# An expert's four activations as one run, beside the last attention unit of layers 1 and 3

## The chip, the core and the metric

The kernel is one program on one core of a Trainium2 chip. It is measured as device time in microseconds (us) of one execution. The engines that matter here each work through a queue of their own in order: PE (matrix products into the PSUM banks), ACT (activation functions, copies out of PSUM), DVE (elementwise work and reductions), POOL and SP (here mostly issuing DMAs). They wait for each other through semaphores.

## What is computed

A token array x of 1024 tokens by 128 features goes through four layers, each a cross attention against a context of 6404 rows and a feed-forward block, both added to x. The two blocks that the change touches are the feed-forward blocks of layers 1 and 3, mixtures of 8 experts that are all computed in full for all tokens:

```
L1:  h = gelu(einsum('bsh,ehf->ebsf', x, w1) + b1)        # E=8, H=128, F=512
     y = einsum('ebsf,efh->ebsh', h, w2) + b2
     out = einsum('ebsh,bse->bsh', y, one_hot(argmax(x @ wr + br)))
...
L3:  h = gelu(einsum('nd,edf->enf', x, w1) + b1)          # 8 experts, D=128, F=512
     res = x + einsum('enf,efd->end', h, w2) + b2
     normed = (res - mean) * rsqrt(var + 1e-6)            # per expert
     y = einsum('end,ne->nd', normed * gamma + beta, gates)   # gates: softmax of the top 2
```

The attention of layers 1 and 3 has 16 heads of 8 features with a softmax over the 6404 context rows.

## The kernel before, in words

The 1024 tokens are handled in two halves of 512. The attention of layers 1 and 3 (`attn_softmax`) runs over 16 units: 8 pairs of heads times two halves. A unit goes through its 51 blocks of 128 keys in 26 steps of two blocks, which makes four score tiles of 128 keys by 512 queries in a step (two blocks, two heads). What is issued in which order is written out by hand: PE, ACT and DVE are in a manual schedule, in which each engine's queue has the order in which the Python code emits the instructions. The order of a step is a string:

```
order = ("SMSMSP", "SMSMP", "SMSMSP")
```

Each letter is a slot. **S** makes scores: by turns an x tile (two score tiles in two banks, one buffer) or a y tile (one bank, one buffer), by the products of L1121, and then their Exp on ACT (L1126, into px or py). An S can be issued on PE only once the Exp of the last tile of its kind has read the bank. **P** multiplies the weights of the step before with the values (L1012). **M** is a slot for other work. In the units before the last it takes the search for the score maxima of a later unit (L893, L897). In the last unit there is no later unit, and M advances two generators instead: `beside` (layer 1 only: the keys of layer 2, `heads_keys`), and from step 9 of the unit on `also`, the feed-forward block of the first half of the tokens, which is ready by then. Each `yield` of that block is the end of an M slot. So the experts of the first half run between the pieces of the last unit, with two M slots to a step; what is left of them is emitted behind the unit's last P, between the pieces of its end (`finish`: copy of the bank at L1020, the division by the softmax sum at L1034, projection).

One call of `expert` does one expert (L1154 on). It asks for a weight tile (two, taken by turns), issues the DMAs of w1 and w2 (L1160, L1161) on SP, and then handles the 512 hidden features in two parts. For each part it makes two first products of 128 features by 512 tokens into banks of `h_tile` (a pool of two buffers in the last unit), each followed by its Gelu on ACT with the bias (L1184), into a hidden tile (two, by turns). In the trace the products are L1183 (two PE instructions each) and the hidden and weight tiles of this place are called kb, since they lie in the storage of the keys' tile. After a `yield`, the function calls what waits in a list; after one more `yield` it puts the part's second products (`second`, L1172: 8 products as 16 PE instructions, summed in one bank of `m_tile`, of which there are two) into that list. The slots of expert e are therefore: part 0; the second part of the second products of expert e-1, and its adding to x on DVE; part 1; the first part of the second products. The adding is `add_weighted` in layer 1 (L627) and `add_normed` in layer 3 (L1702 to L1716, a layer norm per expert, with one power on POOL at L114). With expert 0's adding goes a bias term (`bias`): four transposes (L607), a DVE copy (L608), eight small products (L620) and a DVE add (L614).

ACT holds one set of function tables at a time. Between an Exp and a Gelu, and back, stands an ACT_TABLE_LOAD, which has the line of the activation that needs it.

The second half of the tokens goes through the same `expert` outside the attention (`experts_apart`), with tile pools of three weight and three hidden tiles; no manual schedule is used there.

Of the kernel before, what the change touches and what calls it, by code (L numbers as in the profile page):

```python
# [10 lines left out]
F32 = mybir.dt.float32  # L11
# [4 lines left out]
AF = mybir.ActivationFunctionType  # L16
# [4 lines left out]
P = 128  # L21
S = 1024
NT = S // P
HALF = 512
# [11 lines left out]
def done(steps):  # L36

    while True:
        try:
            next(steps)  # L40
        except StopIteration as end:
            return end.value


class Net:
# [1104 lines left out]

    def expert(self, L, e, xnT, w_tile, hidden_tile, waiting):

        nc = self.nc
        w = w_tile()
        w1, w2 = w[:, :512], w[:, 512:].rearrange("p (k d) -> p k d", d=D)
        nc.sync.dma_start(out=w1, in_=self.a[f"L{L}_ffn_w1"][e])  # L1160
        nc.sync.dma_start(  # L1161
            out=w2, in_=self.a[f"L{L}_ffn_w2"][e].rearrange("(k f) d -> f k d", f=P)
        )
        got = {}

        def second(part, hid):
            if part == 0:
                got["y"] = self.m_tile()
            y = got["y"]
            for i in range(HT):  # L1170
                for k in range(2):
                    nc.tensor.matmul(  # L1172
                        y[:, ts(i, P)], hid[:, k, ts(i, P)], w2[:, 2 * part + k],
                        start=part == 0 and i == 0 and k == 0,
                        stop=part == 1 and i == HT - 1 and k == 1,
                    )

        for part in range(2):
            hid = hidden_tile()
            for j in range(2):  # L1180
                k = 2 * part + j
                h = self.h_tile()
                nc.tensor.matmul(h, w1[:, ts(k, P)], xnT, start=True, stop=True)  # L1183
                nc.scalar.activation(  # L1184
                    hid[:, j], h, AF.Gelu, bias=self.col(f"L{L}_b1", 4 * e + k)
                )
            yield
            while waiting:
                waiting.pop(0)()
            yield  # L1190
            waiting.append(lambda part=part, hid=hid: second(part, hid))
        return got

    def ffn1(self, half, pool, w_tile, hidden_tile):
        nc, a = self.nc, self.a
        E = 8
        wr = pool.tile([P, E], F32, name="wr")
        br = pool.tile([P, E], F32, name="br")
        b2 = pool.tile([E, D], F32, name="b2")
        nc.sync.dma_start(out=wr, in_=a["L1_ffn_wr"])  # L1200
        nc.sync.dma_start(out=br, in_=a["L1_ffn_br"].partition_broadcast(P))
        nc.sync.dma_start(out=b2, in_=a["L1_ffn_b2"])
        xn, xnT = yield from self.normed(half)
        sc = pool.tile([P, HT, E], F32, name="sc")
        nc.vector.tensor_tensor(
            sc, self.router(xnT, wr, E), br.unsqueeze(1).to_broadcast([P, HT, E]), ALU.add
        )
        cw = self.ranks_below(pool, sc, E, 1)
        waiting = []

        def bias():
            self.add_projected(self.weights_transposed(pool, cw, E), b2, half)

        for e in range(E):
            got = yield from self.expert(1, e, xnT, w_tile, hidden_tile, waiting)
            waiting.append(lambda got=got, e=e: self.add_weighted(got["y"], half, cw, e))
            if e == 0:
                waiting.append(bias)
        while waiting:
            waiting.pop(0)()  # L1220
            yield
# [455 lines left out]

    def ffn3(self, half, pool, w_tile, hidden_tile):  # L1680
        nc, a = self.nc, self.a
        E = 8
        wr = pool.tile([P, E], F32, name="wr")
        beta = pool.tile([E, D], F32, name="beta")
        nc.sync.dma_start(out=wr, in_=a["L3_ffn_router_w"])
        nc.sync.dma_start(out=beta, in_=a["L3_ffn_beta"])
        xn, xnT = yield from self.normed(half)
        lg = pool.tile([P, HT, E], F32, name="lg")
        nc.vector.tensor_copy(lg, self.router(xnT, wr, E))
        sel = self.ranks_below(pool, lg, E, 2)  # L1690
        cw = self.exp_shifted(pool, lg, E, "cwr")
        nc.vector.tensor_tensor(cw, cw, sel, ALU.mult)
        self.over_sum(pool, cw, E, "cwsum")
        waiting = []

        def bias():
            self.add_projected(self.weights_transposed(pool, cw, E), beta, half)

        def add_normed(got, e, gb, xb):
            res = pool.tile([P, HT, D], F32, tag="res", name="res", bufs=2)  # L1700
            y = got["y"].rearrange("p (t d) -> p t d", d=D)
            nc.vector.tensor_tensor(res, y, xb, ALU.add)  # L1702
            mv = self.stats(res, HT)
            r = self.rstd(mv[:, :HT, 1], 1e-6, HT)
            rg = self.small.tile([P, NT], F32, tag="rg", name="rg")
            nc.vector.tensor_tensor(rg[:, :HT], r[:, :HT], cw[:, :, e], ALU.mult)
            for t in range(HT):
                nc.vector.tensor_scalar(  # L1708
                    res[:, t], res[:, t], mv[:, t, 0:1], rg[:, t : t + 1],
                    ALU.subtract, ALU.mult,  # L1710
                )
            nc.vector.tensor_tensor(
                res, res, gb[:, :1].to_broadcast([P, HT, D]), ALU.mult
            )
            xs = self.tokens(half)
            nc.vector.tensor_tensor(xs, xs, res, ALU.add)  # L1716

        for e in range(E):

            gb = pool.tile([P, 2, D], F32, tag="gb", name="gb", bufs=2)  # L1720
            nc.sync.dma_start(out=gb[:, 0], in_=a["L3_ffn_gamma"][e].partition_broadcast(P))
            nc.sync.dma_start(out=gb[:, 1], in_=a["L3_ffn_b2"][e].partition_broadcast(P))
            xb = pool.tile([P, HT, D], F32, tag="xb", name="xb", bufs=2)
            nc.gpsimd.tensor_tensor(xb, xn, gb[:, 1:].to_broadcast([P, HT, D]), ALU.add)
            got = yield from self.expert(3, e, xnT, w_tile, hidden_tile, waiting)
            waiting.append(lambda got=got, e=e, gb=gb, xb=xb: add_normed(got, e, gb, xb))
            if e == 0:
                waiting.append(bias)
        while waiting:
            waiting.pop(0)()  # L1730
            yield
# [3 lines left out]
    def run(self, stages):  # L1735
        nc, a = self.nc, self.a
# [4 lines left out]
        with ExitStack() as st:  # L1741
# [33 lines left out]
            def experts(ffn):  # L1775
                def make(stack, scratch):

                    pool = self.pool(stack, "fx")
                    room = scratch[:, : 6 * S].bitcast(F32).rearrange("p (b n) -> p b n", b=3)
                    w = [room[:, 2], pool.tile([P, S], F32, name="w")]  # L1780
                    hid = [room[:, i].rearrange("p (k n) -> p k n", k=2) for i in range(2)]

                    def in_turn(tiles):
                        tiles.append(tiles.pop(0))
                        return tiles[-1]

                    return ffn(0, pool, lambda: in_turn(w), lambda: in_turn(hid))

                return make

            def experts_apart(ffn, stack):
                pool = self.pool(stack, "fy")
                wp = self.pool(stack, "fyw", 3)
                hp = self.pool(stack, "fyh", 3)
                done(
                    ffn(
                        1, pool, lambda: wp.tile([P, 2 * HALF], F32, tag="w", name="w"),
                        lambda: hp.tile([P, 2, HALF], F32, tag="h", name="hid"),
                    )
                )  # L1800

# [52 lines left out]
        if 7 in stages:  # L1854
            with ExitStack() as st:
                self.bank_pools(st, "f3", h=4, m=2)
                experts_apart(self.ffn3, st)
# [99 lines left out]
```

## Time and profile before

Three runs took 8211.31, 8227.63 and 8239.12 us.

| | |
|---|---|
| time, median of 3 runs | 8227.63 us |
| the profiled execution's own time | 8228.82 us |
| its span, first to last instruction | 8227.1 us |
| mean granted PE clock | 0.958 |
| busy: PE, DVE, ACT, POOL | 90%, 76%, 63%, 22% |
| layer 1: first product of expert 0 to the copy at L1020 | 4021.34 to 4115.53, 94.19 us |
| layer 3: the same | 8013.11 to 8119.40, 106.29 us |
| products L1183, activations L1184 (both halves of the tokens) | 256 PE instructions, 128 activations |
| table loads at L1184 and L1126 | 31 and 30, 1283 ns each |

How to read it: busy time is the time in which an engine has an instruction running. A matmul's end is modelled, and matmuls overlap, so the work of PE is better read from the distance between starts. Behind an instruction or a group, in brackets or after the second bar, stands how long the engine was idle just before it and whose instruction ended the idle time. PEclk is the granted clock of PE, 1.00 at full speed. A line of the windows view gives, for a stretch of time, its length and the busy time of PE, PEld (weight loads), DVE, ACT and POOL, each with the number of instructions, then PEclk, the share of the DMA engines and GB/s.

### The profile page before, as it was taken

What the parts mean: (1) busy time and instruction counts of PE and PEld (TensorE: products, weight loads), DVE (VectorE), ACT (ScalarE), POOL (GpSimd) and SP (SyncE); (2) the same over time, 40 slices, a digit from 0 to 9 for tenths busy, and PEclk for the clock granted to TensorE, in tenths of its full rate; (3) what the DMA queues carried; (4) which work ended last, traced back from release to release, by engine and by line L of the source; (5) the groups of instructions that cost most, each with busy time, mean ns of one, the idle gap of its engine ahead of it and who ended that gap; (6) DMA issues with size and microseconds to landing.
All of it is one profiled execution on the core that took longest, in us unless ns stands there. A gap on an engine that the chain in (4) does not pass through costs nothing. (4 is left out here: it accounts for less than half of the span.)

```text
span 8227.1 us, 105455 instructions
## 1 busy us (share of the span) xinstructions
PE 7382.1 (90%) x41959; PEld 2814.9 (34%) x42169; DVE 6271.7 (76%) x7114; ACT 5184.4 (63%) x6033; POOL 1785.2 (22%) x1112
## 2 busy tenths in 40 slices
PE   6999999999999889999978888898888887999997
PEld 2333333333333433333433333322333323333334
DVE  6777777777775578888458888878888878888864
ACT  2444444444445467777748888877788856777765
POOL 4555555555556410000100000000000011000001
PEclk7999999999999899999989999989999988999988
DMA  1000000000000210010310000000000011100101
GB/s 29 1 2 1 2 2 1 2 2 1 1 1 1 73 31 13 14 16 11 115 34 11 12 12 12 12 9 11 10 12 12 12 34 42 16 14 11 19 5 39
DMA packets 145604, 134.97 MB, mean 16 GB/s; under 512 B 31530, under 2 KB 126054, under 8 KB 144206
## 3 DMA queue, kind: packets, MB, share of 16 engines
q1 hardware_dynamic: 134214, 104.37, 5.8%
q0 software_dynamic: 5936, 18.04, 0.7%
q8 instruction: 331, 5.42, 0.3%
q10 hardware_dynamic: 4960, 5.80, 0.2%
q14 instruction: 163, 1.34, 0.1%
HBM read 105.46 MB, written 35.85 MB: 17 GB/s over the span
## 5 line engine op out<-in xcount | busy, mean ns | idle before, releaser
L897 DVE TENSOR_REDUCE mx<-pair_ps 128x2 f32<-128x1024 f32 x1612 | 1810.6, 1177 | 255.6 <-PE pair_ps L893 232.2
L285 DVE TENSOR_REDUCE mx<-b_ps 128x2 f32<-128x1024 f32 x920 | 1091.0, 1186 | 638.2 <-PE b_ps L281 635.6
L331 ACT ACTIVATE pt<-x_ps,bias 128x1024 f32<-128x1024 f32 (+1 forms) x944 | 1001.5, 1111 | 877.3 <-PE x_ps L326 844.2
L345 POOL TENSOR_TENSOR acc<-acc,pt 128x1024 f32<-128x1024 f32 x544 | 1342.7, 2468 | 536.5 <-ACT pt L331 524.0
L1126 ACT ACTIVATE px<-x_ps 128x1024 f32<-128x1024 f32 x1088 | 1114.5, 1024 | 308.0 <-PE x_ps L1121 303.4
L1447 PE MATMUL s_ps<-e,ident 128*128 128x512 f32 (+1 forms) x1632 | 882.5, 623 | 132.4 <-DVE sum L1465 132.2
L1484 DVE TENSOR_TENSOR e<-e,inv 128x1024 f32<-128x1024 f32 (+1 forms) x816 | 991.9, 1216 | 0.0
L1363 ACT CAST lb<-pair_ps 128x1024 bf16<-128x1024 f32 (+1 forms) x714 | 720.5, 1010 | 360.6 <-PE pair_ps L1354 349.7
L351 PE MATMUL o_ps<-pt,v 128*64 128x512 f32 (+1 forms) x3776 | 915.9, 605 | 0.0
L1012 PE MATMUL o_ps<-px,v 128*32 128x512 f32 x4352 | 898.6, 615 | 0.0
L326 PE MATMUL x_ps<-q,kT 64*128 64x512 f32 (+1 forms) x3776 | 894.9, 592 | 0.0
L1012 PE MATMUL o_ps<-py,v 128*32 128x512 f32 x2176 | 891.1, 614 | 0.0
L893 PE MATMUL pair_ps<-kb,qz 64*128 64x512 bf16 (+1 forms) x3224 | 821.8, 384 | 59.0 <-DVE mx L897 33.3
L1439 ACT ACTIVATE e<-x_ps 128x1024 f32<-128x1024 f32 (+1 forms) x816 | 841.2, 1031 | 33.3 <-PE x_ps L1436 31.9
L1126 ACT ACTIVATE py<-y_ps 128x512 f32<-128x512 f32 x1088 | 647.2, 595 | 314.1 <-PE y_ps L1121 312.5
L1121 PE MATMUL x_ps<-qS,kS 33*128 33x512 f32 x2176 | 709.4, 530 | 127.1 <-ACT px L1126 127.0
L345 DVE TENSOR_TENSOR acc<-acc,pt 128x1024 f32<-128x1024 f32 (+1 forms) x368 | 629.9, 1712 | 66.2 <-ACT pt L331 66.1
L1492 PE MATMUL o_ps<-e,vz 128*32 128x256 f32 (+1 forms) x6528 | 546.4, 408 | 59.5 <-DVE vz L1419 55.1
L1121 PE MATMUL y_ps<-qS,kS 33*128 33x512 f32 x1088 | 567.5, 522 | 5.8 <-ACT py L1126 5.8
L1371 DVE TENSOR_TENSOR low<-lb,low 128x1024 bf16<-128x1024 bf16 (+1 forms) x714 | 487.3, 682 | 8.8 <-ACT lb L1363 8.8
L1432 PE MATMUL x_ps<-qS,kS 32*128 32x512 f32 x1632 | 490.0, 594 | 0.0
L1436 PE MATMUL x_ps<-mneg,identb 128*128 128x512 bf16 x1422 | 456.0, 391 | 34.1 <-issue 34.1
(376 smaller groups left out, 8278.3 us busy)
## 6 DMA issues: line engine op xcount, KB each, us to landing
kS<-kst SPq DMA_DIRECT2D x400, 64.0 KB
kS<-kd SPq DMA_DIRECT2D x112, 200.1 KB
w<-in_L_ffn_w SPq DMA_DIRECT2D x48, 256.0 KB
kst<-kd POOLq DMA_DIRECT2D x24, 512.0 KB, 13.8
kd<-kh SPq DMA_DIRECT2D x12, 512.0 KB
kd<-k SPq DMA_DIRECT2D x12, 512.0 KB
qS<-qd SPq DMA_DIRECT2D x256, 16.0 KB
kb<-in_L_ffn_w SPq DMA_DIRECT2D x16, 256.0 KB
```

Of the source, the lines that this page charges most:

```text
L285: nc.vector.tensor_reduce(mxs[u][:, t, :, b], m[:, :, :n], AX.X, ALU.max)
L326: nc.tensor.matmul(s[:n, g], kT[p % 2][r, at : at + n], qs[p][r, ts(half, HALF)], start=False, stop=True,)
L331: nc.scalar.activation(pt[:n], s[:n], AF.Exp, bias=bias[:n, c : c + 1])
L345: eng.tensor_tensor(acc[:n], acc[:n], pt[:n], ALU.add)
L351: nc.tensor.matmul(o[cols], v[:n, c, cols], pt[:n, g], start=c == 0, stop=c == NKT - 1)
L897: nc.vector.tensor_reduce(mxs[u][:, t, b], m[:, :, :n], AX.X, ALU.max)
L1012: nc.tensor.matmul(o[32 * j : 32 * j + 32], v[:, c, ds(VW * h, 32)], pt, start=i == 0, stop=c + 2 >= NK,)
L1121: nc.tensor.matmul(s[:, k], kS[p % 2][r, ts(c, P)], qS[u % 2][r], start=True, stop=True,)
L1126: nc.scalar.activation(pt[:, : len(some)], s[:, : len(some)], AF.Exp)
L1439: nc.scalar.activation(pair(i, k), s[:n], AF.Exp)
L1447: nc.tensor.matmul(firsts[i], self.ident[:n], es[i, h // 4][:n, h % 4], start=h == 0, stop=h == K - 1,)
L1484: nc.vector.tensor_tensor(e, e, r, ALU.mult)
```

## The change

`expert` gets a flag, `grouped`, which `ffn1` and `ffn3` hand through. It is True where the experts run beside the last unit (`experts`) and False for the second half of the tokens (`experts_apart`), whose code stays as it was. With the flag, the slots of expert e are:

1. the first products 0 and 1 (in the same slot as the second part of the second products of expert e-1, since no `yield` lies between them);
2. Gelu 0, first product 2, Gelu 1, first product 3, Gelu 2, Gelu 3; products 2 and 3 take the two banks of products 0 and 1;
3. what waits in the list: the adding of expert e-1, and after expert 0 the bias term;
4. the second products of part 0;
5. (the first slot of expert e+1) the second products of part 1.

The instructions are the same in kind, number and size; only their order and the table loads that follow from it differ.

```diff
-    def expert(self, L, e, xnT, w_tile, hidden_tile, waiting):
+    def expert(self, L, e, xnT, w_tile, hidden_tile, waiting, grouped):
...
+        if not grouped:
+            for part in range(2):
...
+            return got
+
+        hids, banks = [], []
+
+        def first(k):
+            banks.append(self.h_tile())
+            nc.tensor.matmul(banks[k], w1[:, ts(k, P)], xnT, start=True, stop=True)
+
+        for k in range(2):
+            first(k)
+        yield
+        for k in range(4):
+            if k % 2 == 0:
+                hids.append(hidden_tile())
+            nc.scalar.activation(
+                hids[-1][:, k % 2], banks[k], AF.Gelu, bias=self.col(f"L{L}_b1", 4 * e + k)
+            )
+            if k < 2:
+                first(k + 2)
+        yield
+        while waiting:
+            waiting.pop(0)()
+        yield
+        second(0, hids[0])
+        yield
+        second(1, hids[1])
         return got
...
-                    return ffn(0, pool, lambda: in_turn(w), lambda: in_turn(hid))
+                    return ffn(0, pool, lambda: in_turn(w), lambda: in_turn(hid), True)
...
-                        lambda: hp.tile([P, 2, HALF], F32, tag="h", name="hid"),
+                        lambda: hp.tile([P, 2, HALF], F32, tag="h", name="hid"), False,
```

More of the change, by code (lines that the diff above doesn't have):

```diff
@@ L1176, in second, with ffn1 @@
                     )
[L1178 to L1191, printed above, removed]
+        if not grouped:
+            for part in range(2):
+                hid = hidden_tile()
+                for j in range(2):
+                    k = 2 * part + j
+                    h = self.h_tile()
+                    nc.tensor.matmul(h, w1[:, ts(k, P)], xnT, start=True, stop=True)
+                    nc.scalar.activation(
+                        hid[:, j], h, AF.Gelu, bias=self.col(f"L{L}_b1", 4 * e + k)
+                    )
[3 more added lines that the diff above has]
+                yield
+                waiting.append(lambda part=part, hid=hid: second(part, hid))
+            return got
[9 more added lines that the diff above has]
+                hids.append(hidden_tile())
+            nc.scalar.activation(
+                hids[-1][:, k % 2], banks[k], AF.Gelu, bias=self.col(f"L{L}_b1", 4 * e + k)
+            )
+            if k < 2:
+                first(k + 2)
+        yield
+        while waiting:
+            waiting.pop(0)()
+        yield
+        second(0, hids[0])
+        yield
+        second(1, hids[1])
         return got
-    def ffn1(self, half, pool, w_tile, hidden_tile):
+    def ffn1(self, half, pool, w_tile, hidden_tile, grouped):
         nc, a = self.nc, self.a
@@ L1214, in ffn1 @@
         for e in range(E):
-            got = yield from self.expert(1, e, xnT, w_tile, hidden_tile, waiting)
+            got = yield from self.expert(1, e, xnT, w_tile, hidden_tile, waiting, grouped)
             waiting.append(lambda got=got, e=e: self.add_weighted(got["y"], half, cw, e))
@@ L1676, in ffn2, with ffn3 @@
             yield
-    def ffn3(self, half, pool, w_tile, hidden_tile):
+    def ffn3(self, half, pool, w_tile, hidden_tile, grouped):
         nc, a = self.nc, self.a
@@ L1724, in ffn3 @@
             nc.gpsimd.tensor_tensor(xb, xn, gb[:, 1:].to_broadcast([P, HT, D]), ALU.add)
-            got = yield from self.expert(3, e, xnT, w_tile, hidden_tile, waiting)
+            got = yield from self.expert(3, e, xnT, w_tile, hidden_tile, waiting, grouped)
             waiting.append(lambda got=got, e=e, gb=gb, xb=xb: add_normed(got, e, gb, xb))
```

## The prediction

> **What bounds the kernel now.** First the page. PE is busy 90% of the span, ACT 63%, and the chain that ended last runs mostly over PE. These are averages; the change acts only where the experts' code (L1184, L1183, L1172) runs beside the last attention unit of layers 1 and 3, so I cut those stretches out with the windows view: from the first product of expert 0 to the copy out of the unit's bank (L1020) they take 94.19 us (layer 1, from 4021.34) and 106.29 us (layer 3, from 8013.11). Everything below happens in these 200 us, 2.4% of the span.
>
> The groups of ACT show what the change goes for, table loads (functions change between Gelu and Exp):
>
> ```profile
> L1184 ACT ACT_TABLE_LOAD x31 | 39.8, 1283 | 3.4 <-PE h_ps L1183 3.0
> L1126 ACT ACT_TABLE_LOAD x30 | 38.5, 1283 | 15.9 <-PE x_ps L1121 15.4
> ```
>
> Then the timeline of half an expert in the steady part of layer 1 (start, duration, engine, line; brackets: idle before and who ended it):
>
> ```profile
> 4068.50 1.02 ACT L1126 ACTIVATE px<-x_ps 128x1024 f32<-128x1024 f32 x1
> ...
> 4069.09 1.98 PE L1183 MATMUL h_ps<-xnT,w 128*128 128x512 f32 x4
> 4069.40 0.60 ACT L1126 ACTIVATE py<-y_ps 128x512 f32<-128x512 f32 x1
> ...
> 4070.29 1.28 ACT L1184 ACT_TABLE_LOAD   x1 [0.29 <-PE h_ps L1183]
> ...
> 4071.59 1.27 ACT L1184 ACTIVATE kb<-h_ps,cols 128x512 f32<-128x512 f32 x2
> ...
> 4072.85 2.05 PE L1172 MATMUL m_ps<-w,kb 128*128 128x128 f32 x16
> 4072.87 1.28 ACT L1126 ACT_TABLE_LOAD   x1
> 4074.16 1.02 ACT L1126 ACTIVATE px<-x_ps 128x1024 f32<-128x1024 f32 x1
> ...
> 4075.24 0.51 PE L1121 MATMUL x_ps<-qS,kS 33*128 33x512 f32 x2 [0.34 <-ACT px L1126]
> ```
>
> ACT is nearly full, with idle spells of 0.2 to 0.3 us. But so is PE, whose starts I add up from the timeline: a score tile (S, x or y) 0.42 us, the value products of a step (P) 1.00, two first products 1.92, a half of the second products 1.99. Three steps hold 8 S, 3 P, 3 pairs of firsts and 3 seconds: 3.36 + 3.00 + 5.76 + 5.97 = 18.09 us. The trace's three steps (load at 4070.29 to load at 4088.80) take 18.51: PE loses only 0.4 in them, where an S waits for a px as at 4075.24. In the window 4063.09 to 4100.09 PE is busy 36.31 of 37.00 us, ACT 35.32. **Two engines are full at once**, so freeing one buys next to nothing, and any wait that PE gets is paid in full.
>
> **What the change removes.** Four Gelus in one run need two loads per expert where there are four. Of the loads in the two stretches 30 go (31 and 30 become 17 and 14): 30 x 1.283 = 38.5 us of ACT. On the path that is worth what PE loses today: 0.8 us per 37 us, some 2 us a layer.
>
> The Trainium skill ("ScalarE: Activation LUTs", What ACT_TABLE_LOAD costs) puts a switch at 1283 ns plus a drain of about 1380, 2.66 us. The trace has no drain: the Gelu after the load of 4070.29 starts 1.30 after it. By the page, as an estimate, ACT would save 80 us and the new wait below would be 1.38 us longer per expert; the row decides.
>
> **What it adds.** firsts 0 and 1 still start without a wait. first 2 needs the bank of first 0 (h_ps has two buffers), so it stands on PE until Gelu 0 has read it, and Gelu 0 now comes one slot later, behind an Exp and a table load. Behind first 2 in PE's queue stand first 3, the next S, P and the second products; Gelus 2 and 3, the Exps and DVE's adds wait for those. With the durations above (Exp of px: 1.02, next start after 0.92; of py: 0.60 and 0.50; Gelu 0.69 and 0.60; load to next start 1.29; S start to Exp start 0.60; a release 0.06; product end to Gelu 0.24, so first 2 to Gelu 2 1.20) I wrote both queues in program order. Expert 1, from its first 0 at 0.00:
> PE: first 0 at 0.00, first 1 at 0.96, P 1.92, Sy 2.92 to 3.34, **idle to 6.06**, first 2, first 3 7.02, Sx 7.98, Sy 8.40, P 8.82 to 9.82, **idle to 11.28**, Sx, second half 0 at 11.70, Sy 13.69, second half 1 at 14.11, next expert 16.10.
> ACT: idle until the Exp of Sy at 3.52 (PE was busy with products), load 4.02, Gelu 0 5.31 to 6.00, Gelu 1 5.91, Gelu 2 7.26, Gelu 3 8.22, load 8.91, Exp of Sx 10.20 to 11.22, which frees x for the S at 11.28.
> The slots turn through three positions; the others give idle times of 2.72, and of 3.14 + 1.04. Sum of three experts: 2.72 + 1.46 + 2.72 + 3.14 + 1.04 = 11.08, less 2 x 0.40 of today = 10.28 us, **3.43 us per expert**. The same bookkeeping of the code before gives 36.98 for three experts against 37.0 in the trace. Seven of the eight experts have their run inside the stretch: 7 x 3.43 = 24.0 us a layer. The two engines now work in turns: PE's 5.9 us of products leave ACT without a score, and ACT's run leaves PE without a bank.
>
> **What it moves, to the good.** The adds of expert 0 and the bias products leave the slot of second half 1 for one two slots later. Today PE stands there for DVE:
>
> ```profile
> 4041.26 1.15 PE L620 MATMUL m_ps<-b,cT 8*128 8x128 f32 x8 [1.37 <-DVE cT L608]
> ...
> 8043.46 2.07 PE L620 MATMUL m_ps<-beta,cT 8*128 8x128 f32 x8 [6.84 <-DVE cT L608]
> ```
>
> DVE's chain for expert 0 (8036.29 to 8042.73, 6.44 us) will start behind second half 1 as now, but PE will have 8 us of other things before it asks. Layer 3 gets back 6.84, and about 3.3 because what follows ran at half clock (firsts 3.71 instead of 1.92, bias products and scores 1.5 more); the earlier wait for py before 8022.05 (3.47, and 1.8 on the firsts after it) is inside my stalls of expert 0 and comes off too: 15.4. Layer 1 gets back 1.37 + 1.6 = 3.0. Balance at full clock: layer 1 24.0 - 3.0 = +21, layer 3 24.0 - 15.4 = +9.
>
> Tail: behind the last P come a copy (0.6), the load, four Gelus and both second halves: 8.5 us to the end of products, against 7.2 now (ob copy 8119.40 to 8126.6), of which the half moved ahead is already counted; the next link (DVE's add, then the division at 8134.27) hangs on it: +0.8 each, 1.6. The weights' DMAs keep their place on SP and their buffers are read out a slot earlier, so nothing waits for them (today the firsts wait for none); POOL's xb (8118.90) precedes its add (8121.34) and DVE gets no later: nothing. **Full clock: 21 + 9 + 1.6 = +32 us.**
>
> **The clock.** The unknown cost. Rows of before (window, length, PE busy; then DVE, ACT, POOL; PEclk, DMA):
>
> ```profile
> 7999.30:8002.71 3.41, 2.52 (x15) 0.64 (x12) 1.97 (x11) 2.56 (x4) 1.05 (x1) 1.00 0.00 0
> 8002.71:8006.13 3.42, 2.90 (x12) 0.80 (x13) 1.03 (x4) 1.98 (x3) 2.31 (x2) 0.50 0.01 2
> ...
> 8036.85:8040.26 3.41, 0.00 (x0) 0.00 (x0) 2.03 (x12) 0.00 (x0) 1.02 (x1) 1.00 0.26 77
> 8040.26:8043.67 3.41, 0.21 (x1) 0.21 (x2) 3.08 (x7) 0.00 (x0) 0.00 (x0) 0.50 0.03 8
> ```
>
> A stretch of 3.4 us in which PE idles, or has only scores and values with gaps, is followed by half clock for the next; it came back only after a window full of firsts (8047.09 to 8050.50). In the table, 1.92 to 6.06 holds P, one S and 2.72 idle, lighter than the 2.52 busy us that already lost the clock; 7.98 to 11.28 is light again. A window at half clock does 1.71 us less. Ends: none, and three windows an expert, 14 x 3 x 1.71 = 72 us. I take one and a half, since products at half clock stretch over the gaps and some of that is hidden behind ACT: 14 x 1.5 x 1.71 = **36 us**.
>
> The skill ("TensorE: Matmul & The Clock Gate", HAM oscillation) warns only of PE-idle gaps above about 3.4 us; my longest is 3.14. By that rule, as an estimate, the clock would stay up and the sum be +32; the row at 7999.30 fell with no such gap, so I do not use it.
>
> **Sum:** 32 + 36 = +68 us. The profiled execution took 8228.82 us (span 8227.1), 1.2 above the median of 8227.63; 8228.8 + 68 = **8297 us**.
>
> **Rivals.**
> 1. The waits come, the clock holds: 8228.8 + 32 = 8261. For it: the queue table; the rest of this stretch holds full clock today. Chance 0.20.
> 2. The other side, faster: ACT sets the pace and PE has room, so the 38.5 us of loads come off: 8190. For it: ACT idles only 0.2 to 0.3 between its parts and S waits for px in the chain. Place: PE at first 2. It decides where that wait is below about 1.3 us an expert (18.4 us given back over 14 experts); I count 2.7 to 3.1, so Gelu 0 would have to end 1.4 us sooner, with the load out of its way. Against: PE's 18.09 us of work in 18.51. Chance 0.08.
> 3. Gains and waits cancel: the runs ahead of PE and the layer-3 stall are worth more than I count, 8228 to 8250. Chance 0.13.
> 4. The clock stays down most of the time: 32 + 72 = +104, 8333. Chance 0.10; the forecast has 0.49.
> Should something part the Gelus, the loads would stay at 61; no Exp stands between them in the program.
>
> **Numbers.** The range leaves out the faster case and the far ends of 3 and 4: 8240 to 8340. About 0.3% (25 us) is what a measurement of this kernel can tell from no change. Slower by more: forecast, 4 and most of 1: 0.77; within: 3 and the rest of 1: 0.15; faster: 0.08.
>
> **What would show it.** Loads 17 and 14 in the groups; PE idle before L1183's third product about 2.7 us, released by ACT, fourteen times; ACT idle 3 to 4 us per expert for scores; stretches of about 116 us and more where there were 94 and 106; PEclk of 0.5 in them; the 6.84 before L620 gone. I am wrong if PE starts first 2 without that idle time, or if ACT is still full in the stretch.

## The result

Four runs of the changed kernel took 8288.93 to 8302.42 us, median **8293.79**; four of the kernel before 8211.31 to 8239.12, median 8230.85. The ratio is 1.0081 (95% interval 1.0060 to 1.0102): slower, by 63 us. The forecast was 8297 with a range of 8240 to 8340. The profiled execution took 8298.04 us (span 8296.0, mean PE clock 0.953), 68.9 us of span more than the one of before; the forecast had +68.

**The profile after.** First the two stretches, from the first product of expert 0 to the copy at L1020, in the windows view (columns: window, length, busy time of PE, PEld, DVE, ACT, POOL, then PEclk, DMA share, GB/s). Before:

```profile
4021.37:4115.53 94.16, 90.45 (x464) 45.65 (x464) 13.49 (x47) 84.14 (x96) 14.20 (x27) 0.98 0.52 165
8013.18:8119.39 106.21, 94.86 (x461) 47.69 (x462) 36.09 (x126) 84.99 (x97) 12.98 (x12) 0.90 0.13 38
```

After:

```profile
4027.39:4159.76 132.37, 109.79 (x479) 55.14 (x478) 14.72 (x51) 65.44 (x80) 14.18 (x27) 0.82 0.38 117
8045.98:8187.27 141.29, 119.32 (x477) 61.29 (x476) 38.61 (x136) 65.55 (x80) 14.63 (x13) 0.75 0.10 28
```

ACT's busy time fell from 169.1 to 131.0 us, which is what the change went for. The stretches grew from 200.4 to 273.7 us. Of these 73.3 us, 29.5 are idle time of PE (15.1 before, 44.6 after) and 43.8 are busy time (185.3 before, 229.1 after), though PE has the same instructions. The clock column gives the reason for the longer busy time: 2 x (1 - PEclk) x length is the time at half clock (in windows of 3.4 us laid along its steps the column holds 1.00 or 0.50), and with unrounded clocks it went from 23.7 us to 119.5.

The groups of ACT's table loads after:

```profile
L1126 ACT ACT_TABLE_LOAD x16 | 20.5, 1283 | 16.0 <-PE x_ps L1121 15.4
L1208 ACT ACT_TABLE_LOAD x16 | 20.5, 1283 | 0.3
```

With one more at L1186 that makes 33, where there were 61: 28 loads and 35.9 us of ACT went.

The timeline of one expert in layer 1 (L1200 first products, L1208 Gelu, L1173 second products; in brackets the idle time before and who ended it):

```profile
4099.17 1.02 ACT L1126 ACTIVATE px<-x_ps 128x1024 f32<-128x1024 f32 x1 [3.90 <-PE x_ps L1121]
...
4101.37 1.88 PE L1200 MATMUL h_ps<-xnT,kb 128*128 128x512 f32 x4
...
4104.18 0.50 PE L1121 MATMUL y_ps<-qS,kS 33*128 33x512 f32 x1
4104.72 0.60 ACT L1126 ACTIVATE py<-y_ps 128x512 f32<-128x512 f32 x1 [4.52 <-PE y_ps L1121]
4105.33 1.28 ACT L1208 ACT_TABLE_LOAD   x1
4106.63 1.26 ACT L1208 ACTIVATE kb<-h_ps,cols 128x512 f32<-128x512 f32 x2
...
4107.36 3.41 PE L1200 MATMUL h_ps<-xnT,kb 128*128 128x512 f32 x4 [2.68 <-ACT kb L1208]
...
4111.52 1.28 ACT L1126 ACT_TABLE_LOAD   x1
4112.81 1.02 ACT L1126 ACTIVATE px<-x_ps 128x1024 f32<-128x1024 f32 x1
...
4113.89 0.49 PE L1121 MATMUL x_ps<-qS,kS 33*128 33x512 f32 x2 [1.46 <-ACT px L1126]
```

This is the pattern that the prediction wrote out by hand. ACT idles 3.90 and 4.52 us, for scores that PE has not made since it is busy with products. Then PE idles 2.68 us at first product 2, released by Gelu 0, which stood behind the Exp of py and the table load; and 1.46 us at the next scores, behind two more Gelus, a load and an Exp. The first of these waits comes at all fourteen experts of the two stretches: eight of 2.68 or 2.69 us, five of 3.17 or 3.18 and one of 3.94 (expert 0 of layer 3), 41.3 us together. The second is rare: beside the 1.46 us shown, layer 1 has none, and layer 3 has 0.10. The firsts after the wait take 3.41 us where the pair ahead of it took 1.88: they run at half clock. The same stretch of time, window by window:

```profile
4100.04:4103.45 3.41, 3.41 (x21) 2.06 (x24) 1.13 (x4) 0.16 (x1) 0.00 (x0) 1.00 0.17 49
4103.45:4106.87 3.42, 1.23 (x9) 0.18 (x1) 0.00 (x0) 2.12 (x3) 0.00 (x0) 1.00 0.09 28
4106.87:4110.28 3.41, 2.91 (x4) 1.17 (x4) 0.00 (x0) 1.71 (x3) 0.00 (x0) 0.50 0.00 0
4110.28:4113.69 3.41, 2.16 (x13) 0.45 (x11) 0.00 (x0) 2.84 (x3) 0.00 (x0) 1.00 0.30 77
```

The window that holds the wait has 1.23 us of PE work; the next one is granted half the clock, and after it full clock returns.

The products of the bias term, which stood 1.37 us (layer 1) and 6.84 us (layer 3) for DVE:

```profile
4056.70 1.15 PE L620 MATMUL m_ps<-b,cT 8*128 8x128 f32 x8 [0.77 <-DVE cT L608]
...
8080.04 2.07 PE L620 MATMUL m_ps<-beta,cT 8*128 8x128 f32 x8 [0.77 <-DVE cT L608]
```

They wait 0.77 in both layers now: this part of the change does what it was counted to do.

### The profile page after: what moved, and what is told of

It is laid out like the page before. It is cut to its first block, busy times and chain, and to the rows that moved or that the text cites. A ratio compares the mean times of both kernels' runs of the same rounds, so it can differ in the third digit from the quotient of the medians.

```text
span 8296.0 us, 105405 instructions
## 1 busy us (share of the span) xinstructions
PE 7417.7 (89%) x41959; PEld 2830.2 (34%) x42169; DVE 6275.4 (76%) x7114; ACT 5149.0 (62%) x6005; POOL 1782.9 (21%) x1112
## 5 line engine op out<-in xcount | busy, mean ns | idle before, releaser
L1475 PE MATMUL s_ps<-e,ident 128*128 128x512 f32 (+1 forms) x1632 | 884.5, 625 | 132.4 <-DVE sum L1493 132.2
```

Of the source, the lines that this page charges most:

```text
L1475: nc.tensor.matmul(firsts[i], self.ident[:n], es[i, h // 4][:n, h % 4], start=h == 0, stop=h == K - 1,)
```

## The experiments

The theory: PE was full already, so the loads that went bought nothing; the reuse of two banks makes PE wait 2.7 to 3.2 us an expert behind Exp, load and Gelu; and about half of the loss is that wait, the other half the clock that falls behind it. Rival A: the wait alone, and the clock would be the same without it. Rival B: something else on ACT or in the order of the slots, with the wait a symptom. The expectations speak of the **stretches**, the sum of the two windows above, and of half-clock time in them. All runs in one table (ratios are to the runs of the kernel before on the same chip, medians 8223.87 for e1 to e4 and 8225.26 for e5 to e8):

| kernel | layer 1 | layer 3 | sum | at half clock | median | ratio, 95% |
|---|---|---|---|---|---|---|
| before | 94.2 | 106.2 | 200.4 | 23.7 | 8230.85 | |
| after | 132.4 | 141.3 | 273.7 | 119.5 | 8293.79 | 1.0081 (1.0060 to 1.0102) |
| e1_repeat | 118.6 | 116.4 | 235.0 | 15.6 | 8262.34 | 1.0040 (1.0025 to 1.0055) |
| e2_identity_after | 103.4 | 105.4 | 208.8 | 20.4 | 8234.83 | 1.0013 (1.0002 to 1.0024) |
| e3_identity_before | 90.9 | 100.1 | 191.0 | 15.6 | 8223.26 | 0.9992 (0.9980 to 1.0003) |
| e4_second_behind | 109.9 | 115.5 | 225.5 | 49.9 | 8260.21 | 1.0036 (1.0023 to 1.0049) |
| e5_spread | 101.8 | 106.3 | 208.1 | 26.3 | 8238.05 | 1.0018 (1.0007 to 1.0029) |
| e6_bias_first | 94.1 | 94.0 | 188.1 | 15.9 | 8213.86 | 0.9986 (0.9977 to 0.9994) |
| e7_spread_bias | 98.7 | 108.0 | 206.7 | 24.4 | 8244.1, one run | |
| e8_bias_first_warm | 92.6 | 95.2 | 187.8 | 10.2 | 8209.12 | 0.9979 (0.9967 to 0.9991) |

**e1_repeat: fill the gap with useless products.** The changed kernel, with the first product 1 made twice more into its own bank behind the slot's end, where PE would idle:

```diff
         for k in range(2):
             first(k)
         yield
+        for _ in range(2):
+            nc.tensor.matmul(banks[1], w1[:, ts(1, P)], xnT, start=True, stop=True)
```

> The kernel after, with PE given more to do: in the slot of the four Gelus, ahead of them, first product 1 is computed twice again into its own bank (1.92 us of products that change no value), so they fall into PE's idle time of 2.7 to 3.1 us. The two stretches (layer 1 and layer 3, first product of expert 0 to the copy at L1020) take 132.4 + 141.3 = 273.7 us in the kernel after, with the granted clock at half for a good part. Theory (the wait, and the clock that falls because of it): the added work costs nothing, since it fits into the idle time, and keeps the clock up; the stretches fall to 235 to 250 us (232 is the full-clock sum of the queue table), the kernel by 25 to 38 us, to about 8260. Rival A (the wait alone, the clock costs nothing): no change, 274 us, or up to 27 us more if the added products are in the way. Rival B (ACT sets the pace): no change, 274 us.

PE's timeline at one expert, with the repeats at L1206:

```profile
4073.55 1.98 PE L1206 MATMUL h_ps<-xnT,w 128*128 128x512 f32 x4
4076.80 1.98 PE L1200 MATMUL h_ps<-xnT,w 128*128 128x512 f32 x4 [1.27 <-ACT kb L1210]
...
4081.47 0.49 PE L1121 MATMUL y_ps<-qS,kS 33*128 33x512 f32 x1 [1.03 <-ACT py L1126]
```

And the stretches:

```profile
4018.88:4137.53 118.65, 107.28 (x508) 54.50 (x508) 14.68 (x51) 65.23 (x80) 14.17 (x27) 0.96 0.41 131
8034.53:8150.92 116.39, 104.19 (x505) 51.47 (x506) 38.57 (x136) 65.45 (x81) 14.63 (x13) 0.98 0.12 34
```

The repeats (1.98 us) lie inside the old wait: 1.27 of idle time is left behind them, 3.25 together, against 3.18 for this wait in the changed kernel. PE makes 14 times 1.9 us more products, and the stretches are 38.7 us *shorter*, since half-clock time fell from 119.5 to 15.6 us and the firsts behind the wait take 1.98 us where they took 3.41. So the clock's share is about 39 us, and rivals A and B, at 274 and more, fall. At the higher clock the second wait shows: 8.3 us before scores in the two stretches, as the 1.03 above, where the changed kernel has 1.6. There the longer products stood over it. What is left against before, 34.6 us, is the price of the waits at nearly full clock.

**e2_identity_after and e3_identity_before: no table switch at all.** Both leave the Gelu out of the first half of the tokens in layers 1 and 3 (the identity with the bias stands in its place), one in the changed kernel, one in the kernel before:

```diff
-                hids[-1][:, k % 2], banks[k], AF.Gelu, bias=self.col(f"L{L}_b1", 4 * e + k)
+                hids[-1][:, k % 2], banks[k], AF.Identity, bias=self.col(f"L{L}_b1", 4 * e + k)
```

```diff
-                        hid[:, j], h, AF.Gelu, bias=self.col(f"L{L}_b1", 4 * e + k)
+                        hid[:, j], h, AF.Gelu if self.half else AF.Identity, bias=self.col(f"L{L}_b1", 4 * e + k)
```

> The kernel after with Identity in place of Gelu in the run of four (the Gelu is left out in the first half of the tokens of layers 1 and 3): Exp and Identity need no table load between them, so the loads go and all else stays. Theory: Gelu 0 ends 1.29 us sooner and the next Exp another 1.29, so the idle times of PE shrink to about 1.4 and below and the clock holds more often; stretches 206 us at full clock, 210 to 228 with what is left of the clock's falls, kernel 45 to 60 us faster than the kernel after. Rival A (wait alone): 14 waits shorter by 1.29 and no clock: 18 to 36 us less, 238 to 256. Rival B (ACT sets the pace): 30 loads of 1.283 go, 38.5 us less, 235.

> The kernel before with Identity in place of Gelu in the first half of the tokens (the Gelu is left out there): all 60 table loads of the two stretches go, 77 us of ACT. Theory (PE is just as full as ACT): only what PE loses to ACT today goes, some 0.8 us in 37 and the wait of 3.5 us in expert 0 of layer 3: stretches from 200.5 to 188 to 196 us, kernel 5 to 13 us faster than before. Rival B (ACT sets the pace): the stretches lose most of the 77 us, to 125 to 145 us, kernel 55 to 77 us faster.

The decisive one is e3. With every load gone from the stretch, 60 us of its steady part in layer 1 look like this:

```profile
4055.00:4115.00 60.00, 60.00 (x319) 31.53 (x318) 5.63 (x20) 34.62 (x48) 5.27 (x10) 1.00 0.48 156
```

ACT is busy 34.62 of 60 us, PE 60.00 of 60.00, at full clock. Before, with the loads, PE was busy 36.31 of 37.00. So ACT's loads were beside PE's work nearly all the time, and the 57 of the two stretches together were worth 9.4 us of them (200.4 to 191.0; layer 1 alone 3.3) and 0.6 us of the medians. The interval of the ratio takes in 1 and reaches down to 0.9980 (16 us), so the expected 5 to 13 us of the kernel are neither shown nor excluded; the stretches fit (188 to 196), rival B (125 to 145) falls.

In e2 the same wait is shorter by the load:

```profile
4060.67 1.98 PE L1200 MATMUL h_ps<-xnT,kb 128*128 128x512 f32 x4 [1.26 <-ACT kb L1208]
...
4074.21 1.98 PE L1200 MATMUL h_ps<-xnT,w 128*128 128x512 f32 x4 [1.76 <-ACT kb L1208]
```

1.26 and 1.76 where there were 2.69 and 3.18, 1.42 us less: the load that stands between Exp and Gelu 0 was in the wait (from Exp to Gelu 0 it takes 1.91 us at 4104.72 of the changed kernel, and 0.49 at 4059.45 of e2, where no load parts them). Here the clock mostly stays up (20.4 us at half clock), and 208.8 us is all there is, 1.2 below the range expected; the kernel is 59 us faster than the changed one (45 to 60 expected). With shorter waits both shares of the loss shrink at once, 64.9 us for 28 loads of 1.283 (two an expert, one at each wait): a load on PE's path cost nearly twice its length, one beside PE's work (e3, 9.4 us for 57) about an eighth.

**e4_second_behind, e5_spread: fill the gap with real work.** Second half 1 of expert e-1 is held back and issued behind the firsts 0 and 1 of expert e, just ahead of first product 2. In e5 second half 0 moves a slot forward too:

```diff
         for k in range(2):
             first(k)
         yield
+        while self.late:
+            self.late.pop(0)()
...
-        yield
         second(0, hids[0])
         yield
-        second(1, hids[1])
+        yield
+        self.late.append(lambda: second(1, hids[1]))
```

(The lines of e5. e4 leaves the first `yield` where it is and adds none behind `second(0, ...)`. Both empty the list once more behind the last expert.)

> The kernel after with one thing moved: the second products of part 1 of the expert before go from the slot of first products 0 and 1 into the next slot, ahead of the four Gelus, so that PE has 1.99 us of products between the score tile and first product 2. Loads and their number stay as in the kernel after. Theory: PE's idle time before first product 2 falls from 2.72 to about 0.7, and ACT gets its score tile 2 us sooner; full clock 207 us for the two stretches, 212 to 232 with some falls of the clock; kernel 40 to 60 us faster than after. Rival A (wait alone): about 207 against a full-clock sum of 232, so 25 to 28 us less, 246 to 249. Rival B (ACT sets the pace): ACT's work is the same, 274 us.

> The kernel of e4 with one more move: the second products of part 0 go one slot earlier, into the slot of the adds, so that no slot of PE has more than 3.9 us of products and the slot behind the adds is empty. Table loads as in the kernel after. Theory: the idle times before scores (1.0 to 1.5 us in the trace of e4) go as well; full clock 199 us for the two stretches, 200 to 216 with some falls of the clock, against 225.5 in e4 and 200.4 in the kernel before: no gain over before, although 30 table loads are gone, since PE was as full as ACT. Rival A (wait alone): 199. Rival B (ACT sets the pace): the order of PE's work does not matter, 225 us or more, or, once PE's waits are out of the way, 38.5 us less than before, 162.

In e4's timeline of PE (lines one further on) the gap has 1.99 us of products in it:

```profile
4060.71 2.05 PE L1174 MATMUL m_ps<-w,kb 128*128 128x128 f32 x16
4063.47 1.98 PE L1201 MATMUL h_ps<-xnT,kb 128*128 128x512 f32 x4 [0.70 <-ACT kb L1211]
...
4076.65 1.98 PE L1201 MATMUL h_ps<-xnT,w 128*128 128x512 f32 x4 [1.20 <-ACT kb L1211]
```

0.70 and 1.20 us of wait are left where there were 2.69 and 3.18, half-clock time fell to 49.9 us, and the stretches take 225.5, as expected (212 to 232). The kernel came out 33.6 us faster than the changed one, short of the expected 40 to 60. In the two profiles the stretches are 48.2 us shorter and all that lies outside of them is 8.6 us longer (8030.9 against 8022.3), no more than the scatter that e7 shows below. The stretches of e5:

```profile
4019.84:4121.63 101.79, 92.65 (x464) 48.22 (x464) 13.57 (x47) 65.44 (x79) 14.17 (x27) 0.95 0.49 153
8016.14:8122.49 106.35, 94.35 (x461) 48.51 (x462) 36.08 (x126) 65.67 (x81) 13.76 (x12) 0.92 0.13 38
```

They take 208.1 us (expected 200 to 216): 65.6 less than the changed kernel, with the same loads and the same Gelu run. 16.7 of the 41.3 us of waits for Gelu 0 are left. e5 has 28 loads fewer than before, waits for the bias term less (4.4 us in place of 8.2), and still gains nothing: ratio 1.0018 (1.0007 to 1.0029). That is the answer to the change as it was meant: even with most of the wait filled, the loads that went do not pay for what is left of it. It does not tell the theory (200 to 216) from rival A (199) by itself.

**e6_bias_first: only the good part.** The kernel *before*, with only the bias term of the first half moved: into the list ahead of expert 0, so that DVE's copy for it does not stand behind the adding of expert 0:

```diff
+        if half == 0:
+            waiting.append(bias)
...
-            if e == 0:
+            if e == 0 and half:
```

> The kernel before, without the grouping, with one thing moved: the bias term of the first half goes into expert 0's first waiting slot, ahead of expert 0's adds (which it followed). This is the part of the change that I counted to the good, by itself. Theory: the 6.84 us (layer 3) and 1.37 us (layer 1) in which PE waits for DVE's chain go, and with them most of the half clock behind; stretches from 94.2 to 91 to 94 (layer 1) and from 106.2 to 94 to 99 us (layer 3), kernel 8 to 15 us faster, 0.998 to 0.999 of before. Rival (the wait is hidden elsewhere, or comes back behind the next product): under 3 us in the stretches.

```profile
8020.20 1.15 PE L620 MATMUL m_ps<-beta,cT 8*128 8x128 f32 x8 [0.77 <-DVE cT L608]
```

```profile
4028.46:4122.60 94.14, 91.84 (x464) 46.69 (x464) 13.58 (x47) 83.95 (x96) 14.15 (x27) 0.96 0.52 165
8012.39:8106.38 93.99, 92.19 (x461) 46.21 (x462) 36.17 (x126) 84.67 (x97) 12.97 (x12) 0.95 0.14 43
```

Layer 3's stretch falls from 106.2 to 94.0 with all 61 loads in place. Two waits went there: the one for DVE (6.84 to 0.77) and the one of 3.47 us for py before 8022.05, where the bias term's products now stand. The second, in the kernel before:

```profile
8022.05 0.79 PE L1121 MATMUL y_ps<-qS,kS 33*128 33x512 f32 x1 [3.47 <-ACT py L1126]
```

Layer 1's stretch stays (94.1, a hair over the expected 91 to 94, with 6.8 us at half clock instead of 3.4). The kernel is faster than before: 0.9986 (0.9977 to 0.9994). So what the change had to give was in the bias term: with it moved, the stretches take 188.1 us with all loads (e6) and 208.1 with 28 fewer (e5).

**e7_spread_bias** is e5's kernel once more, unchanged, for the scatter of a single profile:

> The kernel of e5 a second time, for one look at how much its two stretches and the time outside of them change from one execution to the next with the clock's windows: stretches within 8 us of e5, the time outside of them within 12 us.

The sum of the stretches differs by 1.4 us (layer 1 by -3.1, layer 3 by +1.7), the rest of the program by 12.2 (8035.6 against 8023.4), just outside the expected 12. So differences of the stretches of well over 3 us can be read from one profile, a difference of spans below about 12 us cannot.

**e8_bias_first_warm: hold the clock ahead of the experts.** In layer 3, ahead of expert 0, the last unit's scores and values run at half clock for a while. e8 is e6 with one useless product of 128 by 512 in each M slot of these steps:

```diff
+                            if u == UNITS - 1 and L == 3 and i < 11:
+                                nc.tensor.matmul(
+                                    self.h_tile(), self.identb, qbf[:, :HALF],
+                                    start=True, stop=True,
+                                )
```

> The kernel of e6 with PE's clock held up ahead of the experts: in layer 3's last unit each of the 22 M slots of steps 0 to 10, empty until the experts start, gets one product of 128 x 128 x 512 in bf16 that nothing reads (22 in all, 0.21 us each at full clock). In the kernel before, 48 us there (7961.76 to 8010.00) ran at a granted clock of 0.54, three steps in 11.65 us where units at full clock take 8.0. Theory (the clock follows what PE does in a window of 3.4 us): these 48 us fall to 33 to 38, so 10 to 15 us less than e6 from the last unit's start to expert 0; kernel 18 to 30 us faster than before, 0.996 to 0.998. Rival (the clock does not follow this, or the scores are bound by ACT there): no change against e6, or 4 us more.

The time from the copy at L1020 of the unit before to the first product of expert 0 in layer 3, of the kernel before:

```profile
7968.46:8013.18 44.72, 41.22 (x144) 13.55 (x145) 5.29 (x18) 22.02 (x29) 3.55 (x3) 0.54 0.01 1
```

of e6:

```profile
7973.76:8012.39 38.63, 35.14 (x145) 12.34 (x145) 5.28 (x18) 21.85 (x30) 3.55 (x3) 0.68 0.01 1
```

and of e8:

```profile
7974.99:8007.84 32.85, 31.65 (x162) 11.12 (x165) 5.29 (x18) 22.55 (x30) 3.55 (x3) 1.00 0.01 2
```

The clock held 1.00, as expected, and these steps take 5.8 us less than in e6, 11.9 less than before, though e8 has 17 more PE instructions in them. That is no luck of one profile: in the nine profiles without the useless products the same steps take 35.5 to 46.0 us at clocks of 0.50 to 0.76. The median, 8209.12, is the best of all (0.9979, 0.9967 to 0.9991, faster than both kernels). It is 16.1 us below before, short of the expected 18 to 30, and only 4.7 us below e6's, where 10 to 15 were expected for these steps; the two can't be told apart. In e6's own profile the clock fell 14 us into these steps, in before's 6.7 us ahead of them, so part of what e8 was to gain e6 had by the luck of that run.

## Why the prediction was right

Its time and its mechanism held: PE full beside ACT, a wait at first product 2, and a clock that falls behind it. Its sum held in part by luck, since errors of size offset each other, in the clock's term and between the stretches and the rest of the program. Step by step:

- **What bounds the kernel: right.** "Two engines are full at once, so freeing one buys next to nothing": e3 took all loads away and PE was busy 60.00 of 60.00 us; e5 took 28 and gained nothing.
- **Loads removed: 30 counted, 28 measured.** 17 at the Gelus as predicted, 16 and not 14 at the Exps: two of these lie outside the stretches, in the layers' starts. As loads cost next to nothing in the kernel before, the error cost little.
- **The first wait: right within 0.05 us.** Predicted 2.72, 2.72 and 3.14 in turn; the seven of layer 1 are 3.17, 2.69, 2.69, 3.18, 2.68, 2.68, 3.18, each ended by Gelu 0, and those of layer 3 the same but for the first (3.94).
- **The second wait: mostly not there.** Predicted 1.46 and 1.04 in three experts, 11.7 us over the fourteen. The changed kernel has 1.6 and e1, at nearly full clock, 8.3: at half clock the longer products stand over it. The prediction took such an overlap off the clock's term instead.
- **ACT's idle time: too small.** Predicted 3 to 4 us an expert for scores; it is 90.4 us in the two stretches, 6.5 an expert.
- **Price at full clock: +21 and +9, measured +24.4 and +10.2** (e1 against before). e1 still has 15.6 us at half clock. At the price of the next point that is some 6 us of its 34.6; an estimate without it is 29, against the 30 predicted.
- **The clock: the sum was right, both factors were not.** Predicted: 1.5 windows an expert at 1.71 us. Half-clock time rose by 95.8 us, 28 windows of 3.41: two an expert. And a window costs less than half of its length: e1 is 38.7 us shorter for 103.9 us less at half clock, 0.37 us for each, 1.27 a window; one reason is the second wait, 6.7 us of which the half clock covered. 95.8 x 0.37 = 35.7 us, against 36 predicted. This agreement is partly luck.
- **What goes: the bias wait, right in its place.** 6.84 became 0.77. e6, with this alone, has 12.2 us less in layer 3; the prediction counted 6.84 + 3.3 for it there, 10.1, and booked the wait of 3.47 for py elsewhere, which e6 loses too. Layer 1's 3.0 did not show in e6 (94.1 against 94.2).
- **The rest of the program: not foreseen.** The stretches grew by 73.3 us, where 39 + 27 = 66 is what the prediction's terms give (24.0 - 3.0 + 18 of clock; 24.0 - 15.4 + 18), and the span by 68.9: outside them 4.4 us went, where +1.6 was predicted. That +68 meets a span that grew by 68.9 rests on these two misses; the medians are 63 us apart. The end behind layer 3's copy grew by 1.0 us. But the part before the experts of layer 3, which the change does not touch, took 35.52 us after and 44.72 before, at mean clocks of 0.76 and 0.54: 9.2 us that belong to the clock of these two executions.

**The rivals.** "The clock holds", 8261: it doesn't; e1, which holds most of it up by useless products, took 8262.34 (a median of four). "ACT sets the pace", 8190: ACT is busy 131.0 of 273.7 us. "Gains and waits cancel", 8228 to 8250: the changed kernel is 44 us above; e5 came out there, at 8238. "The clock stays down most of the time", 8333: 44% of the stretches, and two windows an expert, not three.

**Rules weighed.** In the prediction the row at 7999.30 stood against the rule of the Trainium skill on idle gaps ("TensorE: Matmul & The Clock Gate", HAM oscillation: above about 3.4 us). The changed kernel bears the row out: the longest wait for Gelu 0 in layer 1 is 3.18 us (in layer 3 one of 3.94), and the clock falls. "ScalarE: Activation LUTs" (Rules for kernel authors) of the same notes advises to group activations by table set. The change does that, 28 loads fewer, and is 0.8% slower; e5, which keeps the run and fills the wait, is at 1.0018. Grouping saved ACT's time, 35.9 us, and in the kernel before that time lay beside PE's work.

**When the clock falls.** PE's busy time alone does not decide. A window with 1.23 us of PE work lost it, one with 2.16 us at 4110.28 did not, and one of before with 2.52 did; and the steps ahead of layer 3's experts ran at 0.54 with PE busy 41.22 of 44.72 us. A count over the 24,165 windows of 3.41 us in the ten traces sorts them better. It weights each PE instruction by what its row shows: rows times columns of the array (33 by 128 for a score, 128 by 32 for a value product, 128 by 128 for a first product), times the columns that pass through, bf16 at half weight (which sorts better than full weight). The unit is a window full of first products at 0.48 us for each instruction. Of the windows below 0.40, 1606 of 1743 are followed by half clock, of those from 0.40 to 0.50 455 of 1453, and of those above 4 of 20,969. A limit of 0.46 puts 364 windows on the wrong side; the best limit on busy time, 1422. By that limit the changed kernel's stretches have 33 windows at half clock (35 in the trace), e4's 14 (15), e2's 5 (6) and before's 7 (7). The limit was fitted to these same traces, so it describes them and no run was made to test it. The useless products, which use the whole array, fit it: ahead of layer 3's experts the windows come to 0.45 to 0.72 in e8, and to 0.23 to 0.51 in before.

**What stays open.** The time outside the stretches went from 8022.3 to 8035.6 us over the ten profiles. How much of that is the clock and how much something else was not settled, and with it whether e8 is better than e6.

## What to carry to other kernels

When two engines are full at once, look up what the busier one loses today before freeing the other: here PE lost 0.4 us in 18.5 in the steady part, and taking all loads from ACT (e3) gave 9.4 us of 200. A run of the same function on ACT has its price in the banks: write both queues in program order and see what the in-order PE stands behind when a bank is reused (here Exp, load and Gelu, mostly 2.7 to 3.2 us). Such a wait can be paid a second time through the clock, so fill it with products that are due anyway (e4, e5); and look for the one long wait in the steady part's neighbourhood: here a bias term (6.84 us, two moved lines) gave 12.3 us of the stretches, no less than all the loads.

## What the hardware showed beside this

- Useless products can make a kernel faster: two an expert in e1 shortened the stretches from 273.7 to 235.0 us, and one in each M slot ahead of the experts in e8 held the clock at 1.00 where the same steps had 0.50 to 0.76 in the nine other profiles.
- The length of a wait does not set the clock's loss by itself: waits of 2.7 to 3.2 us went with 119.5 us at half clock in the stretches, as many of 1.26 to 1.76 (e2) with 20.4, but the shorter ones of e4 (mostly 0.70 and 1.20) with 49.9. What the window as a whole asks of the array sorts these cases.
- A busy PE can be at half clock: 92% busy with scores and values, 33 rows or 32 columns wide, it ran at 0.54 (7968.46 to 8013.18 of before).
